# A four-layer graph network on sparse slots: two checks with earlier loads, ScalarE copies for the last groups, and another order of the drain

## The chip, the cores and the metric

The kernel runs on one core of one Trainium2 chip. The metric is the time of one execution on the device in microseconds (us). The time before is 1694.29 us, the median of three runs (1689.37 to 1699.63).

## The reference

There are 128 graphs of 64 nodes with 128 features each (`x`), and an adjacency of 64x64 weights per graph (`adj`), about a quarter of them not zero. Four layers follow each other; each is a graph network whose output is added to its input and normalised over the features.

```python
# layers 0 and 1: a filter per edge
g = exp(coeff * (d_ij - offsets)**2)          # 20 gaussians in layer 0, 64 in layer 1
W = ssp(g @ fw1 + fb1) @ fw2 + fb2            # ssp: softplus less log 2
W = W * weight(d_ij)                          # a cosine cutoff in layer 0, adj itself in layer 1
agg[i] = sum_j (x @ w_in)[j] * W[i, j]
out = ssp(agg @ ow1 + ob1) @ ow2 + ob2
# layer 2: two graph convolutions
h = elu(elu(x @ W0 + b0))
h = elu(nA @ (h @ W1) + b1)                   # nA: adj + 1, scaled by 1/sqrt(degree) on both sides
out = nA @ (h @ W2) + b2
# layer 3
out = relu((nA3 @ x) @ W.T + b)
# after each layer
x = layernorm(x + out)                        # (x - mean) / sqrt(var + 1e-5)
```

## The kernel before, in words

Two graphs make a pair: 128 nodes, one on each partition. Only edges that are there are computed. A node's edges are compacted into slots, the nodes are sorted by their number of edges, and a slot's rows go through memory so that the next step reads them in order. A count decides on the device whether the slots hold all edges; if they do not, another version of the kernel (a dense one, not touched here) runs behind a branch. Everything below is in `sparse_stack`.

**The main loop.** There are 64 pairs, and 128 loop pairs: layer 0 takes pairs 0 to 63, layer 1 pairs 8 to 63 and then 0 to 7. Each has three chunks (`for i in range(3 * N + 2)`, with `n, k = divmod(i, 3)`). For a chunk, TensorE makes the filter's first product `px` (L1753), ScalarE its gaussians and softplus (`d`, `h`), TensorE the second product `pw` (L1766) and the gather `pg` of node features by a one-hot matrix (L1779, `hot` from L1738), ScalarE copies `g` out, VectorE multiplies `m` (L1794), and VectorE sums the segments into `agg` (L1818, L1822). Behind a group of pairs come the node's own layers and a layer normalisation (L1393 to L1415).

**Groups.** Four pairs make a group (`GS`). In layer 1 groups 0 to 13 hold pairs 8 to 63, group 14 holds pairs 0 to 3, group 15 pairs 4 and 5, group 16 pair 6 and group 17 pair 7. Layers 2 and 3 follow for each group in `graph_convs` (L1655 to L1717). In the order of the work its steps are: transpose `gx` and its copy `gxt` (L1664); `gh0` and an `elu` twice over; `hw1` and its copy; `gh1` and an `elu`; `hw2` and its copy; `o2`, the sum `gz2`, a normalisation into `x_all`; `sup` and its copy; `o3`, the sum `gz3` (L1710), a normalisation, and the store. The copies behind `hw1`, `hw2` and `sup` are L1653, the two halves of `elu` are `em` (L1594, the negative part) and `er` (L1595, the positive part), both read from the same accumulator bank. Groups 14 to 17 store by one DMA of SyncE each (L1715); the others scatter four stores from GpSimd (L1719, L1028).

**The normalisation.** Per pair there is a `bn_stats` and a `bn_aggr` on VectorE (L1398, L1399). Then VectorE adds the epsilon to the variances (L1403), and the root is taken: for a group of four on GpSimd by a power of −0.5 (L1406), and for a smaller group on ScalarE by Ln and Exp. The last step, subtract and multiply (L1411), is on GpSimd for a group of four, else on VectorE.

**The order of the work.** Work beside the chunks stands in queues of Python generators; a `yield` ends a step. `run(queue, n)` takes n steps, `slot(queue)` takes one, and a step that has just issued matmuls (`yield True`) lets one more step of its queue follow after the next queue's turn. The queues are:

- `early`: the gathering of layer 1's slots, and at its end two checks (`bounded`), the sum of all checks (`settle`) and the constants of layers 2 and 3 (`late_constants`, among them 16 powers on GpSimd at L1492). It gets twelve steps per loop pair for most of layer 0;
- `side`: `spread_again`, up to two steps a chunk. It loads 16 pieces of a sorted table (`ad0again`, L1068), makes addresses of them on VectorE (`goes`, L1075), scatters rows by them on GpSimd and writes slots;
- `nodes` and two `convs`: the node layers of groups 0 to 14 and their convolutions. At the end of the loop group 14 is in `nodes` and group 13 in one of the `convs`;
- `last`: one queue each for groups 15, 16 and 17;
- `stores`: the scattered stores.

Behind the loop a drain takes what is left in the queues, one turn each: 15, 16, 17, `nodes`, the two `convs`, then one store. `in_order` pins the order of the instructions on every engine as it was written, for the loop and the drain together. So an engine that waits for one instruction holds all that was written behind it.

**Buffers.** The accumulator banks of all this node work come from one ring of two (`ps_n`, tag "n"); `st`, `mv` and `rs` of the normalisation have two buffers each. Every ScalarE activation goes through the helper `act`, and so has line L949.

In `bounded` each of two checks loads a weight and a bias, takes absolute values on VectorE (L1245), sums them by a matmul (L1249) and compares.

Of the kernel before, what the change touches and what calls it, by code (L numbers as in the profile page):

```python
# [12 lines left out]
F32 = mybir.dt.float32  # L13
AF = mybir.ActivationFunctionType
ALU = mybir.AluOpType
# [4 lines left out]
P = 128  # L20
# [6 lines left out]
LN_EPS = 1e-5  # L27
# [574 lines left out]
def sparse_stack(ctx: ExitStack, tc: tile.TileContext, t: dict, out: bass.AP, flag):  # L602
# [11 lines left out]
    nc = tc.nc  # L614
    x, adj = t["x"], t["adj"]
    NB = x.shape[0]
    NP = NB // 2
    GS = 4
    PACE = 4
# [6 lines left out]
    const = ctx.enter_context(tc.tile_pool(name="sconst", bufs=1))  # L626
# [41 lines left out]
    nc.vector.memset(half, 0.5)  # L668
    one = const.tile([P, 1], F32, name="one")
    nc.vector.memset(one, 1.0)  # L670
    neg_one = const.tile([P, 1], F32, name="neg_one")
    nc.vector.memset(neg_one, -1.0)

# [120 lines left out]
    def wait_steps(n):  # L794
        yield from (None for _ in range(n))
# [142 lines left out]
    def act(out_, in_, func, **kw):  # L938
        nonlocal fence, latest, kind
        now = func == AF.Sin  # L940
        if kind is None or now != kind:
            fence = latest
            if not now:
                ctx_ = tc.issue_after(fence.ins) if fence is not None else nullcontext()
                with ctx_:
                    fence = nc.scalar.preload_act_table_set("natural_log_exp_and_others")
            kind = now
        with tc.issue_after(fence.ins) if fence is not None else nullcontext():
            latest = nc.scalar.activation(out_, in_, func, **kw)  # L949
        return latest  # L950
# [276 lines left out]

    def spread_again(s, comb):
        yield from permuted(s, True)
        yield  # L1230
        goes_on(s)
        yield from spread(s, comb)

    def bounded():


        for i, (w, b, k) in enumerate(
            (("L0_gnn_fw1", "L0_gnn_fb1", NG0), ("L1_gnn_W1T", "L1_gnn_b1", NG1))
        ):
            w1 = big(f"w1_{i}", C)[0:k]  # L1240
            nc.sync.dma_start(w1, t[w])
            b1 = const.tile([P, 1], F32, name=f"b1_{i}")
            nc.sync.dma_start(b1, column(b))
            yield from wait_steps(PACE)
            nc.vector.scalar_tensor_tensor(w1, w1, -1.0, w1, ALU.mult, ALU.max)  # L1245
            nc.vector.scalar_tensor_tensor(b1, b1, -1.0, b1, ALU.mult, ALU.max)
            yield from wait_steps(PACE)
            u = ps_n.tile([P, 512], F32, tag="n", name=f"sum_{i}")
            nc.tensor.matmul(u[:, 0:1], lhsT=w1, rhs=one[0:k], start=True, stop=True)  # L1249
            nc.vector.tensor_add(b1, b1, u[:, 0:1])  # L1250
            nc.vector.tensor_scalar(odd[:, 1 + i : 2 + i], b1, X_LIMIT, None, ALU.is_gt)
            yield from wait_steps(PACE)
# [140 lines left out]
    def layernorm(y, dst, n, name):  # L1393

        stats = node.tile([P, GS, 6], F32, tag="st", name=f"st_{name}")[:, 0:n]
        mv = node.tile([P, GS, 2], F32, tag="mv", name=f"mv_{name}")[:, 0:n]
        for s in range(n):
            nc.vector.bn_stats(stats[:, s, :], y[:, s, :])  # L1398
            nc.vector.bn_aggr(mv[:, s, :], stats[:, s, :])  # L1399
            if s + 1 == GS // 2 < n:  # L1400
                yield
        rstd = node.tile([P, GS], F32, tag="rs", name=f"rs_{name}")[:, 0:n]
        nc.vector.tensor_scalar(rstd, mv[:, :, 1], LN_EPS, None, ALU.add)  # L1403
        yield
        if n == GS:
            nc.gpsimd.tensor_tensor(rstd, rstd, neg_half[:, 0:n], ALU.pow)  # L1406
        else:
            act(rstd, rstd, AF.Ln)
            act(rstd, rstd, AF.Exp, scale=-0.5)
        for s in range(n):  # L1410
            (nc.gpsimd if n == GS else nc.vector).tensor_scalar(  # L1411
                dst[:, s, :], y[:, s, :], mv[:, s, 0:1], rstd[:, s : s + 1],
                ALU.subtract, ALU.mult,
            )
        yield  # L1415
# [174 lines left out]
    def elu(ps, bias, i, q):  # L1590

        n = ps.shape[1] // P
        m, r = tiled(f"em{i}", n, q), tiled(f"er{i}", n, q)
        nc.vector.tensor_scalar(m, ps, bias, 0.0, ALU.add, ALU.min)  # L1594
        nc.vector.tensor_scalar(r, ps, bias, 0.0, ALU.add, ALU.max)  # L1595
        yield
        act(m, m, AF.Exp)
        if i == 0:
            act(m, m, AF.Exp, bias=neg_one)
        yield  # L1600
        nc.vector.scalar_tensor_tensor(r, m, 1.0, r, ALU.subtract, ALU.add)
        yield
        return by_pair(r)
# [12 lines left out]
    def normal(i, q, nT):  # L1616
# [7 lines left out]
        dinv = g[f"dinv{i}"][:, pairs]  # L1624
        nc.vector.tensor_mul(nT, ps, dinv.unsqueeze(2).to_broadcast([P, n, P]))

    normals = {}

    def normals_of(q):
# [10 lines left out]
    def graph_convs(q):  # L1640

        pairs = GROUPS[1][q]
        xs = x_all[:, pairs, :]
        n = xs.shape[1]

        def times(name, lhs, rhs):

            _, ps = bank(f"{name}_{q}", n)
            for s in range(n):
                nc.tensor.matmul(ps[:, s, :], lhsT=lhs(s), rhs=rhs(s), start=True, stop=True)  # L1650
            yield True
            y = by_pair(tiled(f"gy_{name}", n, q))
            nc.vector.tensor_copy(y, ps)  # L1653
            yield
            return y  # L1655

        if n == GS:
            scaled(2, q)
        flat, ps = bank(f"gx_{q}", n)
        for s in range(n):  # L1660
            nc.tensor.transpose(ps[:, s, :], xs[:, s, :], ident)
        yield True
        xt = tiled("gxt", n, q)
        nc.vector.tensor_copy(xt, flat)  # L1664
        nc.gpsimd.tensor_tensor(xs, xs, g["b2"].unsqueeze(1).to_broadcast([P, n, C]), ALU.add)
        yield
        flat, _ = bank(f"gh0_{q}", n)
        nc.tensor.matmul(flat, lhsT=g["W0"], rhs=xt, start=True, stop=True)
        yield True
        h = yield from elu(flat, g["b0"], 0, q)  # L1670
        y = yield from times("hw1", lambda s: h[:, s, :], lambda s: g["W1"])
        if n == GS:
            nT = by_pair(tiled("nTs2", n, q))
            yield from normal(2, q, nT)
            yield
        else:
            nT = normals[2, q]
        flat, ps = bank(f"gh1_{q}", n)
        for s in range(n):
            nc.tensor.matmul(ps[:, s, :], lhsT=y[:, s, :], rhs=nT[:, s, :], start=True, stop=True)  # L1680
        yield True
        h1 = yield from elu(flat, g["b1"], 1, q)
        y2 = yield from times("hw2", lambda s: h1[:, s, :], lambda s: g["W2"])
        _, ps = bank(f"o2_{q}", n)
        for s in range(n):
            nc.tensor.matmul(ps[:, s, :], lhsT=nT[:, s, :], rhs=y2[:, s, :], start=True, stop=True)
        if n == GS:
            scaled(3, q)
        yield True
        z = by_pair(tiled("gz2", n, q))  # L1690
        nc.vector.tensor_add(z, ps, xs)
        yield
        yield from layernorm(z, xs, n, f"2_{q}")
        if n == GS:
            nT3 = by_pair(tiled("nTs3", n, q))
            yield from normal(3, q, nT3)
            yield
        else:
            nT3 = normals[3, q]
        y3 = yield from times("sup", lambda s: xs[:, s, :], lambda s: nT3[:, s, :])  # L1700
        flat, ps = bank(f"o3_{q}", n)
        nc.tensor.matmul(
            flat, lhsT=ones, rhs=g["b3"][:, 0:n, :].rearrange("i s c -> i (s c)"),
            start=True, stop=False,
        )
        for s in range(n):
            nc.tensor.matmul(ps[:, s, :], lhsT=y3[:, s, :], rhs=g["W3"], start=False, stop=s == n - 1)
        yield True
        z = by_pair(tiled("gz3", n, q))
        nc.vector.scalar_tensor_tensor(z, ps, 0.0, xs, ALU.max, ALU.add)  # L1710
        yield
        yield from layernorm(z, z, n, f"3_{q}")
        if pairs.start < 8:
            b = 2 * pairs.start
            nc.sync.dma_start(out[b : b + 2 * n].rearrange("(s b) n c -> (b n) s c", b=2), z)  # L1715
        else:
            stores.append(store_rows(pairs, z))  # L1717
# [111 lines left out]

    befores, nodes, convs, sums = deque(), deque(), (deque(), deque()), deque()  # L1830
    small_groups, small = range(NP // GS - 1, len(GROUPS[1])), {}
    last = {q: deque() for q in small_groups}
    stores = deque()
    slot_data, messages, aggs = {}, {}, {}
# [122 lines left out]
        past = [c, c1]  # L1957
    run(sums, -1)
    while nodes or convs[0] or convs[1] or any(last.values()) or stores:
        for queue in (*last.values(), nodes, *convs):  # L1960
            slot(queue)
        run(stores, 1)
    in_order(before_loop, block[-1], (nc.tensor, nc.scalar, nc.vector, nc.gpsimd, nc.sync))

# [46 lines left out]
```

## Time and profile before

| what | value |
|---|---|
| median of three runs | 1694.29 us |
| the profiled execution | 1692.3 us, of it span 1690.4 us |
| PE busy | 1529.1 us (90%) |
| DVE busy | 1509.3 us (89%) |
| ACT busy | 1351.8 us (80%) |
| POOL busy | 721.1 us (43%) |
| mean TensorE clock | 0.966 of full |
| end of the last segment sum (L1822) | 1633.3 us |

PE is TensorE, DVE VectorE, ACT ScalarE, POOL GpSimd and SP SyncE; PEld is TensorE's loading of weights. L1403 is line 1403 of the kernel before. A line of a timeline gives start, length, engine, instruction, tiles and shapes, and in brackets how long the engine had been idle before it and what released it. A line of waits gives the instruction that waited, what released it, the total in us, how many there were and the mean. The page's part 2 cuts the span into 40 slices of some 42 us: a digit is the busy share in tenths, in the row PEclk the granted TensorE clock in tenths. The ends of matmuls are modelled, so a PE that is always busy is not for that reason at its limit.

### The profile page before, as it was taken

How to read it: one execution, taken by the hardware profiler on the slowest of the kernel's cores; microseconds unless marked ns; L12 is line 12 of the kernel's file. 1: busy time of each engine (PE TensorE's matmuls, PEld its weight loads, DVE VectorE, ACT ScalarE, POOL GpSimd, SP SyncE). 2: the span in 40 equal slices, each digit the busy share in tenths (PEclk: the TensorE clock that was granted, in tenths of full speed). 3: DMA queues.
4: the chain of work that ended last, by engine and by line, in shares of the span. 5: the costliest groups of instructions: out<-in, count | busy, mean ns of one | idle time of the engine just before them, and what ended most of it. 6: DMA issues, size and time to landing. Idle time of an engine off the chain costs nothing.

```text
span 1690.4 us, 24016 instructions
## 1 busy us (share of the span) xinstructions
PE 1529.1 (90%) x6813; PEld 790.9 (47%) x6813; DVE 1509.3 (89%) x4125; ACT 1351.8 (80%) x1699; POOL 721.1 (43%) x1119
## 2 busy tenths in 40 slices
PE   1289999999889999998999999999999999998975
PEld 1134444444444444454444555555555555544444
DVE  7689999999979999789888999999999999988875
ACT  1369898989788989697999888898898888887831
POOL 2424455444645433133412354444554444554344
PEclk9999999999989999798999999999999999999986
DMA  7656554556454544344666465555465455465100
GB/s 253 197 127 144 126 139 119 130 125 157 117 123 120 142 114 116 90 130 106 150 149 133 116 144 128 119 134 134 114 141 126 114 133 125 115 143 131 45 6 21
DMA packets 119055, 211.22 MB, mean 125 GB/s; under 512 B 46830, under 2 KB 70656, under 8 KB 118272
## 3 DMA queue, kind: packets, MB, share of 16 engines
q1 hardware_dynamic: 107760, 193.11, 47.6%
q0 software_dynamic: 6576, 14.99, 2.8%
q10 hardware_dynamic: 4576, 1.49, 0.4%
q8 instruction: 56, 0.92, 0.2%
q14 instruction: 87, 0.71, 0.2%
HBM read 190.86 MB, written 18.64 MB: 124 GB/s over the span
## 4 chain that ended last, share of the span: by engine, by line
PE 32%; DVE 11%; issue 8%; POOL 7%; DMA 6%; ACT 4%; SPq 1%; DVEq 0%; POOLq 0%; ACTq 0%
PE pw L1766 11%; PE pg L1779 7%; PE px L1753 6%; DMA out_dram<-gz,at_row 5%; POOL x_all L1411 3%; DVE m L1794 3%; DVE agg L1818 2%; POOL rs L1406 1%; ACT h L949 1%; POOL gz L1411 1%; PE hw L1650 1%; DVE hot L1738 1%; ACT d L949 1%; ACT g L949 1%; PE back L1577 1%
## 5 line engine op out<-in xcount | busy, mean ns | idle before, releaser
L949 ACT ACTIVATE g<-pg 128x672 f32<-128x672 f32 (+12 forms) x384 | 298.8, 778 | 134.3 <-PE pg L1779 129.4
L949 ACT ACTIVATE h<-h,half 128x672 f32<-128x672 f32 (+13 forms) x385 | 351.1, 912 | 12.5
L1779 PE MATMUL pg<-hot,ys 64*128 64x336 f32 (+12 forms) x1536 | 352.6, 537 | 4.7 <-ACT g L949 4.6
L1818 DVE TENSOR_REDUCE agg<-m 128x16 f32<-128x240 f32 (+13 forms) x896 | 324.8, 410 | 2.4
L1766 PE MATMUL pw<-h,w_L_gnn_fw 128*128 128x336 f32 (+6 forms) x768 | 279.6, 489 | 38.9 <-DVE m L1794 38.8
L1766 PE MATMUL pw<-h,w_L_gnn_W2T 128*128 128x420 f32 (+5 forms) x768 | 303.1, 517 | 3.0 <-DVE m L1794 3.0
L1794 DVE SCALAR_TENSOR_TENSOR m<-pw,c_L_gnn_b,g 128x420 f32<-128x420 f32 (+5 forms) x384 | 226.0, 625 | 10.9 <-PE pw L1766 8.1
L1794 DVE SCALAR_TENSOR_TENSOR m<-pw,c_L_gnn_fb,g 128x336 f32<-128x336 f32 (+6 forms) x384 | 201.9, 564 | 25.9 <-PE pw L1766 19.6
L949 ACT ACTIVATE h<-px,c_L_gnn_b 128x840 f32<-128x840 f32 (+5 forms) x192 | 176.8, 921 | 44.6 <-PE px L1753 44.3
L1779 PEld LDWEIGHTS pg<-hot,ys 64*128 64x128 f32 x1536 | 118.6, 189 | 187.3 <-ACT h L949 98.9
L1766 PEld LDWEIGHTS pw<-h,w_L_gnn_fw 128*128 128x128 f32 x768 | 138.6, 199 | 135.8 <-DVE m L1794 84.7
L1753 PE MATMUL px<-d,fw 32*128 32x336 f32 (+6 forms) x768 | 170.8, 522 | 29.5 <-ACT d L949 28.6
L1766 PEld LDWEIGHTS pw<-h,w_L_gnn_W2T 128*128 128x128 f32 x768 | 133.1, 191 | 129.3 <-DVE m L1794 32.3
L1406 POOL TENSOR_TENSOR rs<-rs,neg_half 128x4 f32<-128x4 f32 x61 | 67.8, 1111 | 276.8 <-DVE rs L1403 275.4
L1738 DVE SCALAR_TENSOR_TENSOR hot<-j,row,w 128x1212 f32<-128x1212 bf16 (+12 forms) x128 | 175.7, 1373 | 8.8 <-DMA w<-w_dram 8.8
L949 ACT ACTIVATE h<-px,c_L_gnn_fb 128x672 f32<-128x672 f32 (+6 forms) x192 | 158.3, 824 | 20.8 <-PE px L1753 15.6
L1753 PE MATMUL px<-d,w1t 64*128 64x420 f32 (+5 forms) x768 | 169.8, 519 | 0.0
L949 ACT ACTIVATE d<-d,neg_off 128x1212 f32<-128x1212 f32 (+12 forms) x128 | 136.4, 1065 | 8.0 <-DMA d<-d_dram 8.0
L1028 POOL DMA_INDIRECT rows<-comb,goes x64 | 68.9, 1076 | 117.7 <-DMA rows<-comb,goes 75.9
L1753 PEld LDWEIGHTS px<-d,fw 32*128 32x128 f32 x768 | 60.3, 191 | 124.8 <-issue 46.9
L1411 POOL TENSOR_SCALAR x_all<-ny,mv,rs 128x128 f32<-128x128 f32 x124 | 108.5, 881 | 3.4
L1028 POOL DMA_INDIRECT out_dram<-gz,at_row x56 | 71.3, 1273 | 50.5 <-DMA out_dram<-gz,at_row 39.8
(261 smaller groups left out, 2206.6 us busy)
## 6 DMA issues: line engine op xcount, KB each, us to landing
d<-d_dram SPq DMA_DIRECT2D x32, 315.0 KB
w<-w_dram SPq DMA_DIRECT2D x32, 315.0 KB
d<-d_dram SPq DMA_DIRECT2D x32, 303.0 KB
w<-w_dram SPq DMA_DIRECT2D x32, 303.0 KB
w<-w_dram SPq DMA_DIRECT2D x32, 252.0 KB
j<-j_dram SPq DMA_DIRECT2D x32, 157.5 KB
j<-j_dram SPq DMA_DIRECT2D x32, 151.5 KB
d<-d_dram SPq DMA_DIRECT2D x16, 300.0 KB
```

The source lines that it names most:

```text
L949: latest = nc.scalar.activation(out_, in_, func, **kw)
L1028: nc.gpsimd.indirect_dma_start(out=into, out_offset=bass.IndirectOffsetOnAxis(ap=at, axis=0), in_=rows, in_offset=None,)
L1406: nc.gpsimd.tensor_tensor(rstd, rstd, neg_half[:, 0:n], ALU.pow)
L1411: (nc.gpsimd if n == GS else nc.vector).tensor_scalar(dst[:, s, :], y[:, s, :], mv[:, s, 0:1], rstd[:, s : s + 1], ALU.subtract, ALU.mult,)
L1577: nc.tensor.matmul(ps[:, s, :], lhsT=back[:, s, :], rhs=o[:, s, :], start=True, stop=True)
L1650: nc.tensor.matmul(ps[:, s, :], lhsT=lhs(s), rhs=rhs(s), start=True, stop=True)
L1738: nc.vector.scalar_tensor_tensor(hots[n][:, 0:size], j[:, 0:size], near, wt[:, 0:size], ALU.is_equal, ALU.mult)
L1753: nc.tensor.matmul(ps[:, b, 0:n], lhsT=w["w1"][rows, :], rhs=d[rows, col : col + n], start=True, stop=True,)
L1766: nc.tensor.matmul(ps[:, 0 : c["size"]], lhsT=c["w"]["w2"], rhs=c["h"][:, b, :], start=True, stop=True)
L1779: nc.tensor.matmul(ps[:, b, 0:n], lhsT=y[rows, :], rhs=hots[c["n"]][rows, at], start=True, stop=True,)
L1794: nc.vector.scalar_tensor_tensor(messages[n][:, b, at], c["pw"][b][:, 0:size], c["w"]["b2"], c["g"][:, b, :], ALU.add, ALU.mult,)
L1818: nc.vector.tensor_reduce(av[:, :, :, r], both, AX.X, ALU.add)
```

## The change

Five edits, without any in the number of matmuls, loads or stores:

1. `spread_again` lets four steps pass between its loads and `goes`, not one.
2. `bounded` issues the loads of both checks first, lets 32 steps of `early` pass, and then makes the two checks, with eight steps between the absolute values and the sum, not four. It takes 56 steps, not 24, and what stands behind it in `early` moves back.
3. The addition of the epsilon leaves VectorE. For groups of four GpSimd does it, ahead of its power; for smaller groups it is the bias of ScalarE's Ln, from a constant tile. The 70 instructions of L1403 become 61 on GpSimd.
4. For groups 14 to 17 (`at_end`) the four copies (`gxt`, `hw1`, `hw2`, `sup`) and the positive half of both `elu` go from VectorE to ScalarE: 24 instructions.
5. In the drain, the queue of group 17 has a turn ahead of each other queue that isn't empty, and one more at the end of each round.

```diff
     def spread_again(s, comb):
         yield from permuted(s, True)
-        yield
+        yield from wait_steps(4)
         goes_on(s)
         yield from spread(s, comb)
 
     def bounded():
+        loaded = []
         for i, (w, b, k) in enumerate(
             (("L0_gnn_fw1", "L0_gnn_fb1", NG0), ("L1_gnn_W1T", "L1_gnn_b1", NG1))
         ):
...
             nc.sync.dma_start(b1, column(b))
-            yield from wait_steps(PACE)
+            loaded.append((w1, b1))
+        yield from wait_steps(8 * PACE)
+        for i, (w1, b1) in enumerate(loaded):
             nc.vector.scalar_tensor_tensor(w1, w1, -1.0, w1, ALU.mult, ALU.max)
             nc.vector.scalar_tensor_tensor(b1, b1, -1.0, b1, ALU.mult, ALU.max)
-            yield from wait_steps(PACE)
+            yield from wait_steps(2 * PACE)
             u = ps_n.tile([P, 512], F32, tag="n", name=f"sum_{i}")
...
         rstd = node.tile([P, GS], F32, tag="rs", name=f"rs_{name}")[:, 0:n]
-        nc.vector.tensor_scalar(rstd, mv[:, :, 1], LN_EPS, None, ALU.add)
         yield
         if n == GS:
+            nc.gpsimd.tensor_scalar(rstd, mv[:, :, 1], LN_EPS, None, ALU.add)
             nc.gpsimd.tensor_tensor(rstd, rstd, neg_half[:, 0:n], ALU.pow)
         else:
-            act(rstd, rstd, AF.Ln)
+            act(rstd, mv[:, :, 1], AF.Ln, bias=ln_eps)
             act(rstd, rstd, AF.Exp, scale=-0.5)
...
         nc.vector.tensor_scalar(m, ps, bias, 0.0, ALU.add, ALU.min)
-        nc.vector.tensor_scalar(r, ps, bias, 0.0, ALU.add, ALU.max)
+        if q in at_end:
+            act(r, ps, AF.Relu, bias=bias)
+        else:
+            nc.vector.tensor_scalar(r, ps, bias, 0.0, ALU.add, ALU.max)
...
+    def copy(to, ps, q):
+        if q in at_end:
+            act(to, ps, AF.Copy)
+        else:
+            nc.vector.tensor_copy(to, ps)
...
-            nc.vector.tensor_copy(y, ps)
+            copy(y, ps, q)
...
-        nc.vector.tensor_copy(xt, flat)
+        copy(xt, flat, q)
...
     small_groups, small = range(NP // GS - 1, len(GROUPS[1])), {}
+    at_end = range(NP // GS - 2, len(GROUPS[1]))
...
     while nodes or convs[0] or convs[1] or any(last.values()) or stores:
-        for queue in (*last.values(), nodes, *convs):
-            slot(queue)
+        longest = last[small_groups[-1]]
+        for queue in (*list(last.values())[:-1], nodes, *convs):
+            if queue:
+                slot(longest)
+                slot(queue)
+        slot(longest)
         run(stores, 1)
```

More of the change, by code (lines that the diff above doesn't have):

```diff
@@ L670, in sparse_stack @@
     nc.vector.memset(one, 1.0)
+    ln_eps = const.tile([P, 1], F32, name="ln_eps")
+    nc.vector.memset(ln_eps, LN_EPS)
     neg_one = const.tile([P, 1], F32, name="neg_one")
@@ L1243, in bounded @@
             nc.sync.dma_start(b1, column(b))
-            yield from wait_steps(PACE)
+            loaded.append((w1, b1))
+        yield from wait_steps(8 * PACE)
+        for i, (w1, b1) in enumerate(loaded):
             nc.vector.scalar_tensor_tensor(w1, w1, -1.0, w1, ALU.mult, ALU.max)
             nc.vector.scalar_tensor_tensor(b1, b1, -1.0, b1, ALU.mult, ALU.max)
-            yield from wait_steps(PACE)
+            yield from wait_steps(2 * PACE)
             u = ps_n.tile([P, 512], F32, tag="n", name=f"sum_{i}")
-            nc.tensor.matmul(u[:, 0:1], lhsT=w1, rhs=one[0:k], start=True, stop=True)
+            nc.tensor.matmul(u[:, 0:1], lhsT=w1, rhs=one[0 : w1.shape[0]], start=True, stop=True)
             nc.vector.tensor_add(b1, b1, u[:, 0:1])
```

## The prediction

> **What bounds the kernel now.** I read the page first, then the waits by engine, the busy time by stage, and the timeline at the few places where an engine stands still.
>
> ```profile
> PE 1529.1 (90%) x6813; PEld 790.9 (47%) x6813; DVE 1509.3 (89%) x4125; ACT 1351.8 (80%) x1699; POOL 721.1 (43%) x1119
> ...
> PEclk9999999999989999798999999999999999999986
> ...
> PE 32%; DVE 11%; issue 8%; POOL 7%; DMA 6%; ACT 4%; SPq 1%; DVEq 0%; POOLq 0%; ACTq 0%
> ```
>
> TensorE and VectorE are both near 90%, and the clock row dips at slices 12 and 17 and at the end. The busy time by stretch (columns: window; length, PE, PEld, DVE, ACT, POOL busy with instructions; clock, DMA share, GB/s) tells the stages apart:
>
> ```profile
> 480.00:500.00 20.00, 15.11 (x66) 7.26 (x64) 12.99 (x38) 15.03 (x19) 8.61 (x11) 0.83 0.63 144
> 695.00:720.00 25.00, 22.76 (x91) 11.03 (x90) 17.38 (x47) 17.23 (x24) 0.96 (x1) 0.80 0.28 69
> 1000.00:1200.00 200.00, 199.77 (x928) 106.53 (x928) 187.75 (x427) 174.37 (x204) 90.19 (x97) 1.00 0.55 127
> 1632.00:1684.00 52.00, 34.18 (x147) 24.57 (x147) 36.08 (x127) 9.91 (x33) 21.40 (x26) 0.70 0.05 14
> ```
>
> In the steady loop (row 3) PE shows 199.8 of 200 us and DVE 187.8; PE's ends are modelled, and in the timeline it keeps being released by DVE's product `m` (L1794), so I take DVE as the tight engine there. Rows 1 and 2 are two short stalls; row 4 is the tail, where nothing is full and a chain decides.
>
> **The two stalls.** The timeline has them (columns: start, length, engine and instruction, then the idle time before it and its releaser):
>
> ```profile
> 488.70 0.23 DVE L1075 TENSOR_SCALAR goes<-ad0again,row 128x8 uint32<-128x8 f32 x1 [6.76 <-DMA ad0again<-perm_again]
> ...
> 490.06 2.61 PE L1766 MATMUL pw<-h,w_L_gnn_fw 128*128 128x336 f32 x4 [4.89 <-DVE m L1794]
> ```
>
> ```profile
> 697.95 0.28 DVE L1245 SCALAR_TENSOR_TENSOR w<-w 20x128 f32<-20x128 f32 x1 [4.69 <-DMA w<-in_L_gnn_fw_dram]
> 698.29 0.30 PE L1249 MATMUL sum<-one,w 20*128 20x1 f32 x1 [2.24 <-DVE w L1245]
> 699.65 2.58 PE L1766 MATMUL pw<-h,w_L_gnn_fw 128*128 128x332 f32 x4
> ```
>
> DVE takes its queue in order, so a `goes` or a `w` that waits for its load holds the `m` behind it. After the gap the same four matmuls take 2.61 and 2.58 us; at 482.33 they took 1.30.
>
> **What the Trainium skill says.** "TensorE: Matmul & The Clock Gate", Part 1 (HAM clock gate): after an idle window of about 3.4 us PE runs at half clock until about 3.4 us of activity. The trace agrees: 1.30 to 2.61 us after an idle of 4.89, and to 2.58 at the second stall. "Perfetto Trace Analysis", Optimizing Scalar/DVE Operations: each DVE or ScalarE instruction has a fixed access overhead; work may be moved from a saturated DVE to ScalarE, but between GpSimd and DVE it may not help, since they share an SBUF port. The trace shows the overhead (128x4 add, 0.2 us a slot); the port sharing it doesn't show. "PSUM — Partial Sum Buffer", PSUM bank collisions: accesses of one bank by two engines must be serialised. The trace agrees: DVE's `nh` (L1556) waits 38.9 us in 24 cases for ScalarE's `na` on the same bank.
>
> **The change, part by part.** Sums are against the profiled execution, 1692.3 us (span 1690.4, 1.9 around it); it lies 2.0 under the shown median of 1694.3.
>
> *Checks further ahead.* `goes<-ad0again` goes about three chunks later (some 12 us at about 4 us a chunk), `w` eight chunks later: both exceed the 6.76 and 4.69 us by which the loads were late. SP's sixteen loads (5.67 us of issue) keep their place, and DVE work of the next chunks covers them. The scatters, row loads and stores behind `goes` move by up to a pair (13 us); POOL's `dinv` powers (16, last start 822.5) move by up to three chunks, and their first use is at 897.6. First stall: stepping through the order without that wait, the `m` that came at 493.06 could come at about 487.2: 5.9 us. Cover against it: ScalarE's two table loads (1.28 us each, 483.4 and 485.1) in the same gap, so 2.6 less at worst. Second: 2.24 us of PE idle, plus some 5.3 us that PE's groups take longer at half clock until 708 (L1766 1.3 more, L1779 and L1753 0.65 more a group), less what DVE makes up: 6. Sum −12 (−6 to −16).
>
> *L1403.* By shape, 61 adds of 128x4 are busy 20.1 us, mean 329 ns (a few long ones); by start times one occupies 0.2 us of DVE: from an aggregate (1245.86) over its add (1246.08) to the next instruction (1246.16) it is 0.30, and 0.10 where no add follows (1628.10 to 1628.20). 56 of the 61 lie in the loop: 56 × 0.2 = 11.2. The group of four pairs is DVE-paced, but not everywhere: I take −9 (0 if PE is the limit, to −14 where slots are 0.25). POOL gets 61 adds ahead of the power. That form isn't in the trace; POOL's small TENSOR_SCALARs (L1094, 128x13) have a median of 0.25, its 128x128 one 0.78: I take 0.4 and both as bounds. POOL has 90 of 200 us, so in the loop it is hidden; in the tail five of them lie on the chain. The small groups' add goes into ScalarE's Ln: nine DVE slots of 0.08 to 0.2, near nothing.
>
> *Copies and `er` on ScalarE.* 24 instructions leave DVE in the tail: gxt .68+.41+2×.28, `er` 2×(.74+.47+2×.34), hw 2×(.69+.42+2×.28), sup .69+.39+2×.28, in all 10.6 us, to a ScalarE with 9.9 of 52 us busy. `er` now waits for `em` (same bank) and the exponential behind it comes 0.3 to 0.6 later; for a chain this is nearly neutral. It frees DVE, which the drain uses: counted below. One wait is new on DVE: group 16's third mean takes one of two `mv` buffers, which POOL's `x_all` of group 14 gives back; behind it on DVE stands group 14's last stage, which needs that `x_all` too, so I cost it at nothing (up to 3 us, one POOL normalisation, if it catches group 16's end).
>
> *The drain.* In the built order all of the last pair's work (queue 17) now stands ahead of group 13's last norm on DVE, ScalarE and PE. Before, from the last segment sum (L1822, ending 1633.3) to that norm it was 16.6 us:
>
> ```profile
> 1649.88 1.03 POOL L1406 TENSOR_TENSOR rs<-rs,neg_half 128x4 f32<-128x4 f32 x1 [2.12 <-DVE rs L1403]
> ...
> 1666.49 3.19 POOL L1411 TENSOR_SCALAR x_all<-gz,mv,rs 128x128 f32<-128x128 f32 x4
> ...
> 1670.57 0.69 DVE L1653 COPY gy_sup<-sup 128x512 f32<-128x512 f32 x1 [3.10 <-PE sup L1650]
> ...
> 1677.86 1.03 POOL L1406 TENSOR_TENSOR rs<-rs,neg_half 128x4 f32<-128x4 f32 x1 [8.18 <-DVE rs L1403]
> 1679.00 3.12 POOL L1411 TENSOR_SCALAR gz<-gz,mv,rs 128x128 f32<-128x128 f32 x4
> ```
>
> From there POOL runs a chain of its own to the end, 40.5 us: group 13's four normalisations and four stores (3.2 us apart), group 14's power, its `x_all`, PE's sup, o3, its second power and `gz`, then the store. Queue 17 alone, summed over its rows: DVE 6.9, ScalarE 4.1, PE some 5.5 (eleven stages at 0.4 to 0.8), with 33 handovers of 0.05 to 0.1: 19 to 20 us, and with the work of others between, 21 to 26. So group 13's norm comes +5 to +10 later. What follows gets shorter by about 3: the copy of sup beside DVE, and 17's end (DVE's 1.47 wait, ln, `gz`, 1683.4) no longer behind POOL. The last sum itself ends 1 earlier (gxt copies of .68 and .41 gone from in front). Adds on POOL: +1. +7 −3 −1 +1 ≈ +4 to +5. I take +5 (−4 to +9). What ends last then is group 14 through POOL.
>
> Sum: −12 −9 +5 = −16, hence 1676 for the profiled execution and about 1678 for the median.
>
> **Rivals.** (a) *The loop is PE-bound.* For: 199.8 of 200. Against: its ends are modelled, and it waits 41.8 us for `m`. Then L1403 gives 0, the stalls about 6, the tail takes 5: 1693, no change. (b) *The tail gains.* For: 17 was last, 10.6 us leave DVE. Against: POOL's 40.5 us hold no 17. If group 13's norm doesn't move and the −3, −1 stand with 4 more: −12 −9 −8 → 1665. (c) *Slower.* The turns of 17 put group 13's norm, and with it POOL's serial chain, behind 17's handovers at half clock (0.70 here): 14 later instead of 7, tail +12, and the loop gives 3 or less: 1703. It decides where the tail's loss is over the loop's gain by 8.5. (d) *The checks still wait*, because layer 1's `goes` meets other late loads: −12 becomes −3, so 1687: no change.
>
> **Chances.** Forecast (1670 to 1686) 0.5; (b) 0.14; (a) and (d) 0.21; (c) 0.15. Faster, by over 0.5%, which is about what can be told from no change, means under 1685.8: 0.5 and 0.14, less the forecast's edge: 0.63; same 0.22; slower 0.15. The range leaves (c) and a little of (b) out: 1664 to 1697.
>
> **What would show it.** No wait of DVE for `ad0again` or `w`, and a clock near 1.0 in slices 12 and 17; L1403 gone from DVE and the groups of four pairs in the loop shorter by 0.2 us a norm; 17's store ahead of group 13's and POOL's last `gz` ending last; a tail of about 62 us from the last sum, against 57.1. Wrong would be: a loop of the old length, a new wait of POOL or DVE in the loop, or a tail over 66 us.

## The result, and the profile after

The changed kernel takes 1687.75 us (median of 18 runs), the kernel before 1698.0 us over as many. The ratio is 0.9942, 95% interval 0.9921 to 0.9962: about 10 us are gained, where 16 were forecast. The time lies just above the forecast of 1670 to 1686 and within the wider 1664 to 1697; the sum does not hold, since its terms are off in both directions. The profiled execution has a span of 1686.6 us, against 1690.4.

The page of the changed kernel, the lines that answer to those shown of before (line numbers in a view are those of the kernel that it shows):

```profile
PE 1517.6 (90%) x6813; PEld 788.5 (47%) x6813; DVE 1480.2 (88%) x4032; ACT 1359.3 (81%) x1723; POOL 737.2 (44%) x1180
...
PEclk9987999999989999999999999999999999999965
...
PE 46%; DVE 22%; DMA 9%; ACT 7%; POOL 7%; issue 5%; SPq 2%; another core or an unknown queue 1%; DVEq 0%; POOLq 0%; ACTq 0%
```

DVE has 93 instructions and 29 us less. The clock row's dips in slices 17 and 19 are gone, that in slice 12 is not; slices 3 and 4 and the last two are slower. The two checks no longer wait for their loads.

To see where the time went I cut the execution by loop pairs: the start of each pair's one-hot instruction (`hot`) in DVE's timeline marks them, the end of the last `agg` marks the last segment sum, and the tail is the rest of the span. Lengths in us:

| kernel | pairs 0-8 | 8-34 | 34-38 | 38-50 | 50-56 | 56-60 | 60-64 | 64-120 | 120 to last sum | tail |
|---|---|---|---|---|---|---|---|---|---|---|
| before | 99.0 | 289.4 | 50.9 | 129.1 | 72.1 | 38.1 | 49.3 | 695.7 | 133.8 | 57.1 |
| changed | 106.6 | 280.6 | 51.1 | 128.6 | 61.8 | 38.3 | 46.8 | 697.0 | 129.8 | 70.1 |

The 75.9 us ahead of pair 0 are the same in both. Before the last sum 16.8 us are gained, although pairs 0 to 8 took 7.6 more. I leave these pairs out, since they do not follow the change: of the executions below, with the edits and without them, some show 94 to 99 us there and others 102 to 108. The tail loses 13.0.

Much of what differs between the two rows is PE's clock. The same stretches, as the time in us for which the clock stood at one half (worked out from the granted clock of windows of some 4 us, as length × 2 × (1 − clock)):

| kernel | pairs 0-8 | 8-34 | 34-38 | 38-50 | 50-56 | 56-60 | 60-64 | 64-120 | 120 to last sum | tail |
|---|---|---|---|---|---|---|---|---|---|---|
| before | 3.4 | 13.7 | 13.6 | 3.4 | 17.1 | 0 | 13.7 | 0 | 13.3 | 36.6 |
| changed | 27.3 | 0 | 17.0 | 0 | 3.5 | 0 | 3.4 | 0 | 11.3 | 56.5 |

From pair 8 to the last sum that is 74.8 us before and 35.2 changed. The same four matmuls take 2.61 us at half clock and 1.30 at full clock, so 39.6 us less at half clock are worth up to 20 us, by estimate, of the 24.4 that these stretches gained. So a wait that goes can save more than its own length: the slow matmuls behind it go too.

**The tail.** POOL's and SP's lines of the changed kernel's timeline, from its last segment sum at 1616.5 on:

```profile
1643.77 0.34 SPq L1730 DMA_DIRECT2D out_dram<-gz  x1
...
1646.15 0.23 POOL L1410 TENSOR_SCALAR rs<-mv 128x4 f32<-128x4 f32 x1 [3.48 <-DVE mv L1404]
1646.47 1.04 POOL L1411 TENSOR_TENSOR rs<-rs,neg_half 128x4 f32<-128x4 f32 x1
...
1663.04 1.05 POOL L1411 TENSOR_TENSOR rs<-rs,neg_half 128x4 f32<-128x4 f32 x1
1664.19 3.13 POOL L1416 TENSOR_SCALAR x_all<-gz,mv,rs 128x128 f32<-128x128 f32 x4
...
1673.68 0.23 POOL L1410 TENSOR_SCALAR rs<-mv 128x4 f32<-128x4 f32 x1 [6.36 <-DVE mv L1404]
```

Queue 17's store is issued first, 27.3 us after the last sum, and group 13's last norm begins right behind it, at 29.6 us where it was 16.6. From there to the end it is 40.4 us, and it was 40.5: POOL's chain has moved as a whole.

**The first check.** The stretch of pairs 34 to 38 gained nothing in this execution, though DVE no longer waits for `ad0again`:

```profile
483.90 3.16 SPq L1070 DMA_DIRECT2D ad0again<-perm_again  x8
...
487.18 1.42 SPq L1290 DMA_DIRECT2D d<-d_dram  x3
...
490.55 0.85 ACT L951 ACTIVATE d<-d,neg_off 96x672 f32<-96x672 f32 x1 [4.15 <-DMA d<-d_dram]
...
492.07 1.11 PE L1794 MATMUL pg<-hot,ys 64*128 64x336 f32 x4 [3.90 <-ACT g L951]
...
494.52 2.61 PE L1781 MATMUL pw<-h,w_L_gnn_fw 128*128 128x336 f32 x4
```

SP issues the loads of `d` behind those of `ad0again`. ScalarE waits 4.15 us for `d` (1.92 in the kernel before), PE stands still for 3.90, and its clock halves as it did before (2.61 for the four matmuls). This wait alone did not eat the gain. The same kernel with the old drain (e1 below) has nearly the same wait, and its stretch takes 45.8 us. Its lines:

```profile
490.86 0.86 ACT L951 ACTIVATE d<-d,neg_off 96x672 f32<-96x672 f32 x1 [3.86 <-DMA d<-d_dram]
...
492.38 1.49 PE L1794 MATMUL pg<-hot,ys 64*128 64x336 f32 x4 [3.61 <-ACT g L951]
...
499.75 1.40 PE L1781 MATMUL pw<-h,w_L_gnn_fw 128*128 128x336 f32 x4
```

In the changed kernel the same matmuls are still slow much later:

```profile
507.15 2.45 PE L1781 MATMUL pw<-h,w_L_gnn_fw 128*128 128x336 f32 x4
```

The clock was back at about 499 in e1, after 6.8 us, and at about 509 in the changed kernel, after 17.0, although PE's row has no gap there from 492 on. Why it took so much longer is open.

### The profile page after: what moved, and what is told of

Same layout as the page of the kernel before. It is cut to its first block, busy times and chain, and to the rows that moved or that the text cites. A ratio compares the mean times of both kernels' runs of the same rounds, so it can differ in the third digit from the quotient of the medians.

```text
span 1686.6 us, 24029 instructions
## 1 busy us (share of the span) xinstructions
PE 1517.6 (90%) x6813; PEld 788.5 (47%) x6813; DVE 1480.2 (88%) x4032; ACT 1359.3 (81%) x1723; POOL 737.2 (44%) x1180
## 4 chain that ended last, share of the span: by engine, by line
PE 46%; DVE 22%; DMA 9%; ACT 7%; POOL 7%; issue 5%; SPq 2%; another core or an unknown queue 1%; DVEq 0%; POOLq 0%; ACTq 0%
PE pw L1781 16%; PE pg L1794 9%; PE px L1768 9%; DVE m L1809 6%; DMA out_dram<-gz,at_row 5%; DVE agg L1833 3%; ACT h L951 2%; POOL gz L1416 2%; DVE hot L1753 2%; PE y L1441 2%; ACT g L951 2%; POOL x_all L1416 2%; DMA w<-w_dram 1%; ACT d L951 1%; DVE at L1179 1%
## 5 line engine op out<-in xcount | busy, mean ns | idle before, releaser
L1781 PE MATMUL pw<-h,w_L_gnn_fw 128*128 128x336 f32 (+6 forms) x768 | 273.1, 479 | 29.3 <-DVE m L1809 26.5
L1410 POOL TENSOR_SCALAR rs<-mv 128x4 f32<-128x4 f32 x61 | 25.9, 425 | 266.8 <-DVE mv L1404 265.5
L1416 POOL TENSOR_SCALAR x_all<-ny,mv,rs 128x128 f32<-128x128 f32 x124 | 104.9, 855 | 3.3
L1768 PEld LDWEIGHTS px<-d,w1t 64*128 64x128 f32 x768 | 68.6, 187 | 49.3 <-issue 11.9
```

What stands on the lines that cost most here:

```text
L1410: nc.gpsimd.tensor_scalar(rstd, mv[:, :, 1], LN_EPS, None, ALU.add)
L1416: (nc.gpsimd if n == GS else nc.vector).tensor_scalar(dst[:, s, :], y[:, s, :], mv[:, s, 0:1], rstd[:, s : s + 1], ALU.subtract, ALU.mult,)
L1768: nc.tensor.matmul(ps[:, b, 0:n], lhsT=w["w1"][rows, :], rhs=d[rows, col : col + n], start=True, stop=True,)
L1781: nc.tensor.matmul(ps[:, 0 : c["size"]], lhsT=c["w"]["w2"], rhs=c["h"][:, b, :], start=True, stop=True)
```

## The experiments

My theory after the result had four parts: the drain's turns cost the tail 10 us and more by putting off group 13's norm; the checks give the loop's gain; the moved addition gives nothing in layer 1, since PE paces it; the ScalarE copies give nothing. The rivals stand with each run. Lengths of stretches, tails and times at half clock come from one profiled execution of each kernel. Ratios are to the kernel before, with their 95% intervals.

**Old drain (e1).** The changed kernel with the drain of before:

```diff
-        longest = last[small_groups[-1]]
-        for queue in (*list(last.values())[:-1], nodes, *convs):
-            if queue:
-                slot(longest)
-                slot(queue)
-        slot(longest)
+        for queue in (*last.values(), nodes, *convs):
+            slot(queue)
```

> The changed kernel with the drain's order of before; the other four edits stay. Theory (the turns of queue 17 put its chain ahead of group 13's last norm, and with it the whole POOL chain): from the last segment sum to the end of the span it is about 56 us again, where the changed kernel has 70.1 and the kernel before 57.1; the time is about 13 us under the changed kernel's, ratio to the kernel before about 0.986. Rival (the loss of the tail comes from `er` waiting for `em` on another engine, the ScalarE copies and POOL's added step): the tail stays at 68 to 70 us and the ratio at 0.994.

The tail is 58.1 us and the ratio 0.9882 (0.9839 to 0.9925). Group 13's norm comes at 17.2 us after the last sum, and 41.0 follow:

```profile
1633.35 0.23 POOL L1410 TENSOR_SCALAR rs<-mv 128x4 f32<-128x4 f32 x1 [1.45 <-DVE mv L1404]
```

So the drain's order gives away some 10 us of what the rest of the change gains.

**Drain alone (e8).** The kernel before with the reverse of that edit.

> The kernel before with the new drain alone. Theory: the tail goes from 57.1 to 67 to 71 us, with the loop as before: ratio 1.006 to 1.008. Rival (the turns cost only together with the ScalarE copies, which wait for `em`): the tail stays under 61 us, ratio 1.000 to 1.002.

The tail is 67.9, the norm comes at 27.8, the ratio is 1.005 (1.0029 to 1.007). The turns cost without the ScalarE copies too. In all, the five executions with this drain have tails of 67.9 to 70.1 us (the changed kernel, e2, e4, e5 and e8), and the five with the old drain and POOL's norms 57.1 to 60.6 (the kernel before, e1, e3, e6 and e9).

**Extra turns only behind group 13 (e12).** The changed kernel with:

```diff
             if queue:
-                slot(longest)
+                if not convs[1]:
+                    slot(longest)
                 slot(queue)
```

> The changed kernel, but queue 17's extra turns begin only once group 13's queue is empty; until then each queue has one turn. Theory (the loss comes from group 13's last norm standing behind queue 17's chain, so POOL's chain begins late): that norm comes again about 17 us after the last segment sum and the tail takes 56 to 60 us, ratio 0.988. Rival (the extra turns cost by their handovers wherever they stand, or delay group 14 just as much): the tail stays at 66 to 70 us, ratio 0.994.

The norm comes at 15.6 us, the tail is 60.6, the ratio 0.9866 (0.9826 to 0.9906). So it is the place in front of group 13's norm that costs most. A smaller part of the rival is seen too, as POOL's next norm in this kernel shows:

```profile
1642.95 0.23 POOL L1410 TENSOR_SCALAR rs<-mv 128x4 f32<-128x4 f32 x1 [5.47 <-DVE mv L1404]
```

POOL now waits for group 14's mean, which the extra turns delay; from group 13's norm to the end it is 45.0 us, not 41.

**Checks alone (e3).** The kernel before with edits 1 and 2.

> The kernel before with edits 1 and 2 alone (both checks' loads further ahead). Theory (all that the loop gained comes from the second check and what moved with it; the first check's stall was replaced by ScalarE's wait for `d`): 12 to 16 us less than before, ratio 0.991 to 0.993; the tail stays at 57 us; in the stretch of loop pairs 34 to 50 nothing is gained. Rival (half of the loop's gain comes from DVE's relief): 5 to 8 us less, ratio 0.996.

The ratio is 0.9896 (0.9858 to 0.9934), a gain of some 18 us (11 to 24), which has room for the theory's 12 to 16. But one part of the expectation falls: pairs 34 to 38 take 46.2 us, not 50.9. Of all kernels with edit 1, only the profiled execution of the changed one shows no gain there (the others take 43.5 to 47.7 us, with 3.4 to 10.2 at half clock). Pairs 50 to 56 take 60.5 (72.1 and 68.2 in the two executions without edit 2), with no time at half clock (17.1 and 10.3), and pairs 60 to 64 take 47.3 (49.3). The tail is 60.6, not 57.

**Second check alone (e9).** The kernel before with edit 2.

> The kernel before with edit 2 alone (the check of the weights). Theory (the first check is worth about 5 us, the second 10 and more): loop pairs 34 to 38 take 51 us as before, where they take 44 to 46 with edit 1; pairs 50 to 56 take 60 to 63, against 72.1; ratio 0.992 to 0.994, against 0.990 with both edits. Rival (edit 1 is worth nothing, since ScalarE's wait for `d` takes the stall's place): the ratio equals that of both edits, 0.990.

The ratio is 0.9957 (0.994 to 0.9974), pairs 34 to 38 take 49.7, and 50 to 56 take 61.9. Edit 2 is worth about 7 us, and edit 1 the difference to 0.9896: some 10, with an uncertainty of about 7. The ratio is above the 0.992 to 0.994 expected: the theory had given the second check the larger share.

**Loads two to a step (e4).** The changed kernel with a `yield` between the pairs of loads:

```diff
             for k in range(8):
+                if again and k:
+                    yield
                 for h in range(2):
```

> The changed kernel, but the sixteen loads of `ad0again` (and of `ad1again`) are issued two to a step, not sixteen at once, so that SyncE can issue the loads of the next pairs' `d` between them. Theory (SyncE's queue, held by the sixteen loads and their scatters, had delayed `d`; ScalarE's 4.15 us wait for it took the place of DVE's 6.76): that wait falls under 1 us, PE keeps its clock, and 4 to 8 us are gained on the changed kernel, ratio 0.990 to 0.992. Rival (the transfer itself is late, not its issue, or another wait follows): the ratio stays at 0.994.

A miss: ScalarE's wait for `d` is gone in pairs 34 to 38, but they take 46.6 us, no less than 45.8 with the old drain alone, and the ratio is 0.9971 (0.9951 to 0.999). Another wait came instead: at 479 us PE stands still for 3.27 for an `agg` of the node layers, and its clock is at one half for 6.8 us, as long as in e1. So the run does not tell what the order of issue alone is worth there. Pairs 8 to 34 take 291.8 us, where the other kernels with the addition on POOL take 280.4 to 280.8. PE is at half clock for 20.5 of these 291.8 and for none in the others, which by estimate is 10 of the 11 us; why the spread loads bring this about stays open.

**Addition back on DVE (e2).** The changed kernel with L1403 in its old place:

```diff
+        nc.vector.tensor_scalar(rstd, mv[:, :, 1], LN_EPS, None, ALU.add)
         yield
         if n == GS:
-            nc.gpsimd.tensor_scalar(rstd, mv[:, :, 1], LN_EPS, None, ALU.add)
             nc.gpsimd.tensor_tensor(rstd, rstd, neg_half[:, 0:n], ALU.pow)
         else:
-            act(rstd, mv[:, :, 1], AF.Ln, bias=ln_eps)
+            act(rstd, rstd, AF.Ln)
```

> The changed kernel with the addition of the epsilon back on DVE, in its old place, for all groups. Theory (layer 1's loop is paced by PE, which hardly ever waits for `m` there; the 61 adds had been free): the stretch of layer 1 from loop pair 64 to 120 is as long as in the changed kernel within 2 us, and the ratio stays at 0.994. Rival (DVE paces it): that stretch grows by 8 us and the ratio goes to 0.999.

Pairs 64 to 120 take 695.4 us, against 697.0 with the addition on POOL, and 695.1 to 700.0 in all executions but e5's, on whichever engine it is: the 37 adds were free there. The ratio is 0.9965 (0.9943 to 0.9988), in between and apart from neither. What there is lies elsewhere: pairs 8 to 34 take 284.1 (280.6), pair 120 to the last sum 134.6 (129.8). In layer 0 PE does wait for `m`, a little longer with the addition on DVE, and in one place its clock then halves. The same four matmuls in e2 and, with the addition on POOL, in e1:

```profile
411.11 2.64 PE L1781 MATMUL pw<-h,w_L_gnn_fw 128*128 128x340 f32 x4 [1.44 <-DVE m L1809]
```

```profile
409.25 1.41 PE L1781 MATMUL pw<-h,w_L_gnn_fw 128*128 128x340 f32 x4 [1.02 <-DVE m L1809]
```

Pairs 8 to 34 have 3.4 us at half clock in e2, and none with the addition on POOL (e4 apart).

**A matmul twice (e5).** The changed kernel with layer 1's `u` issued twice for groups of four:

```diff
-        nc.tensor.matmul(
-            u, lhsT=w["o1"], rhs=agg.rearrange("f s r -> f (s r)"), start=True, stop=True
-        )
+        for _ in range(1 + (layer == 1 and n == GS)):
+            nc.tensor.matmul(
+                u, lhsT=w["o1"], rhs=agg.rearrange("f s r -> f (s r)"), start=True, stop=True
+            )
```

> The changed kernel, with the first matmul of layer 1's node layers (`u`, 128x512, 0.59 us) issued twice for the 15 groups of four; the second overwrites the first with the same values. About 13 of them lie between loop pairs 64 and 120: 7.7 us more for PE, nothing more for DVE. Theory (PE paces layer 1's loop): that stretch, 697.0 us in the changed kernel and 695.7 in the kernel before, grows by 6 to 8 us and the whole by 8 to 9, ratio 0.999. Rival (DVE paces it, or both have slack behind some latency): the stretch stays within 2 us and the ratio at 0.994.

Pairs 64 to 120 take 707.3 us, 10.3 more, and the ratio is 0.9999 (0.9972 to 1.0025). That is more than the 7.7 expected: a group's `u` is two records of together 1.12 us, and doubled it takes 1.98, so the thirteen in this stretch add 11.2. PE paces layer 1: its added work shows almost in full, DVE's did not. The page of the kernel before had said so, in two lines of its costliest groups (the last columns: idle time before them, and who ended it):

```profile
L1766 PE MATMUL pw<-h,w_L_gnn_fw 128*128 128x336 f32 (+6 forms) x768 | 279.6, 489 | 38.9 <-DVE m L1794 38.8
L1766 PE MATMUL pw<-h,w_L_gnn_W2T 128*128 128x420 f32 (+5 forms) x768 | 303.1, 517 | 3.0 <-DVE m L1794 3.0
```

`fw` is layer 0's weight, `W2T` layer 1's. Of PE's 41.8 us of waits for `m`, 38.8 are in layer 0.

**Copies back on DVE (e6).** The changed kernel with the old drain and `at_end` empty:

```diff
-    at_end = range(NP // GS - 2, len(GROUPS[1]))
+    at_end = ()
```

> The changed kernel with the drain of before and with the last groups' copies and `er` on DVE as before; what is left of the change is the checks and the moved addition. Theory (in the tail DVE's 10.6 us were no limit; POOL's chain is): the tail from the last segment sum stays at 57 to 60 us as in the run with the old drain alone (58.1), ratio 0.987 to 0.990. Rival (the copies on ScalarE did help by some 5 us): the tail is 62 us or more and the ratio 0.991 or more.

The tail is 60.5 us, against 58.1, and the ratio 0.9878 (0.9847 to 0.9909), against 0.9882. The copies are worth nothing that can be told: DVE had 25.7 us of work in the 50.8 from the last sum on in e1, and the two tails also differ in their time at half clock (50.4 and 44.4).

**Last norms off POOL (e10).** The changed kernel with the old drain, and:

```diff
+        on_pool = n == GS and name not in ("3_13", "2_14", "3_14")
         yield
-        if n == GS:
+        if on_pool:
...
-            (nc.gpsimd if n == GS else nc.vector).tensor_scalar(
+            (nc.gpsimd if on_pool else nc.vector).tensor_scalar(
```

> The changed kernel with the drain of before, and the last norm of group 13 and both last norms of group 14 done as the small groups' are (Ln and Exp on ScalarE, the last step on DVE), not on POOL. Theory (POOL's serial chain sets the tail; DVE takes 0.3 us a pair where POOL takes 0.8, and group 14 no longer waits for group 13's stores): the tail goes from 58 to 49 to 53 us, ratio 0.983 to 0.985. Rival (another chain, that of queue 17 or of group 14 through PE at half clock, ends as late): 56 us or more, ratio 0.987 to 0.988.

The tail is 52.9 us and the ratio 0.9813 (0.9777 to 0.9849), the lowest of all: 1656 us, where the kernel before took 1690 beside it. The interval of e1 reaches down to 0.9839, so the time alone does not part the two; the tail, shorter than the 57.1 to 60.6 of the five above, does. The theory's way is seen in part: group 14's norm does not get past group 13's stores but still comes behind the last of them, the first line below, and what is shorter is the step itself:

```profile
1641.09 0.96 POOL L1030 DMA_INDIRECT out_dram<-gz,at_row  x1 [2.08 <-DVE gz L1726]
...
1642.21 1.11 DVE L1417 TENSOR_SCALAR x_all<-gz,mv,rs 128x128 f32<-128x128 f32 x4 [0.86 <-ACT rs L951]
...
1652.97 1.11 DVE L1417 TENSOR_SCALAR gz<-gz,mv,rs 128x128 f32<-128x128 f32 x4 [0.17 <-ACT rs L951]
...
1656.79 0.35 DVE L1417 TENSOR_SCALAR gz<-gz,mv,rs 128x128 f32<-128x128 f32 x1 [0.60 <-ACT rs L951]
```

Four pairs take DVE 1.11 us, where POOL took 3.13, twice over, and group 14's last stage is done at 1654.1, which is 44.2 us after the last sum, against 49.8 in e1; what ends last now is a small group again. PE was at half clock for only 29.0 us of this tail (44.4 in e1), and what part of the 5 us that is, the run does not show.

**Groups 13 and 14 first in a round (e11).** As e10, with `for queue in (*convs, nodes, *last.values())`.

> As the run before it (three norms off POOL), with the drain's turns in the order convs, nodes, then queues 15, 16, 17. Theory (groups 13 and 14 set the end, so their turn should be first in a round): one more turn's lead, 1 to 3 us less, ratio 0.982 to 0.985. Rival (a round's order doesn't matter, since every queue has one turn in it): the same as the run before it.

A miss: the tail is 54.7 us, the ratio 0.9842 (0.9804 to 0.9881), no better than e10. A round's order is not worth a turn, as the rival said.

## Why the prediction was off, point by point

Two steps of the prediction failed: that DVE is the tight engine of the steady loop, and that queue 17 puts group 13's norm off by only 5 to 10 us. A third term, that of the checks, was too small. Of the signs of being wrong that the prediction named, a tail over 66 us came (70.1).

- *Two checks, −12 forecast.* The mechanism holds, the size was low: −17.7 by the time of both alone (0.9896 of 1698.0). 7 are the second check's, where 6 were forecast. The first gives more than the 5.9 of its stall; part of it lies in pairs 8 to 34, which take 284.6 with both edits and 286.8 to 290.9 without edit 1. The sum priced only the wait for `ad0again`, and for this check none of the slow matmuls behind a wait: without edit 1 PE is at half clock for 6.9 to 13.7 us in pairs 8 to 34 and for 13.6 in pairs 34 to 38, with both edits alone for 3.4 and 6.8. Edit 1 also moves the `goes` of `ad1again`, which begins at 185.0 before and 202.7 after; that this makes the difference in pairs 8 to 34 I have not tested. A gain of 2 at pairs 60 to 64 wasn't foreseen either (46.6 to 47.3 us with edit 1, but 50.0 in e1; 49.3 without).
- *L1403, −9 forecast.* The step "I take DVE as the tight engine there" failed. The −9 priced the 56 adds of the loop as if DVE paced nearly all of it, from a wait summed over both layers. PE paces layer 1, and the 37 adds of pairs 64 to 120 gave 0. What the addition gives (0.9942 against 0.9965, 4 us with an uncertainty of more than 4) shows in layer 0 and the last pairs. Rival (a) was right on this term, but not on the stalls.
- *POOL's added step, 0.4 assumed:* it took 0.23 us in the lines above and 0.425 in the mean of all 61, a few being long, and no loss shows in the loop.
- *ScalarE copies:* the forecast put no number to them but in the −3 behind the norm. The chain from POOL's `rs` of group 14 to its next got 1.6 us shorter (12.52 to 10.95), and the stores ahead of it 1.1 longer (15.46 to 16.57 between the powers): 40.4 for 40.5. The −3 was not there. The sum of the 24 instructions, given as 10.6 us, is 10.4 by its own terms; nothing hangs on it.
- *The drain, +5 forecast for the tail, +13.0 measured.* The mechanism was right: group 13's norm stood behind queue 17, and POOL's chain began later. The term "+5 to +10 later", taken at 7, was too small; it was 13.0, near the mechanism of rival (c), which had 14. The loop's gain covered it: that the total still came within 6 us of the forecast is luck, since errors of both signs met.

Why 27.3 us for queue 17, which I had at 19 to 20 alone and 21 to 26 with others between? Two lines of busy time, from the last sum to group 13's norm, before and changed (columns as in the prediction):

```profile
1633.30:1649.90 16.60, 12.10 (x64) 8.60 (x64) 12.20 (x39) 4.81 (x14) 1.27 (x3) 0.89 0.01 1
```

```profile
1616.50:1646.20 29.70, 20.43 (x82) 15.12 (x82) 13.93 (x44) 11.42 (x34) 2.98 (x6) 0.61 0.01 2
```

DVE did 1.7 us more in 13.1 us more, PE 8.3 more, and its clock fell from 0.89 to 0.61. A chain of one pair leaves the engines idle at each handover, and between two turns of queue 17 there still is one of another queue, in order, with instructions four pairs wide. In the changed kernel's timeline:

```profile
1629.15 1.91 PE L1665 MATMUL sup<-nTs,x_all 128*128 128x128 f32 x8
1630.86 0.64 PE L1695 MATMUL gh<-small,gy_hw 128*128 128x128 f32 x2
1631.10 0.69 DVE L1640 COPY gy_sup<-sup 128x512 f32<-128x512 f32 x1 [1.80 <-PE sup L1665]
1631.71 0.34 DVE L1599 TENSOR_SCALAR em<-gh,c_L_gnn_b 128x128 f32<-128x128 f32 x1
```

Queue 17's `gh` waits behind 1.91 us of another group's `sup`, and its `em` behind the copy of that. The prediction had taken PE's stages at 0.4 to 0.8 us and the handovers at 0.05 to 0.1; the order's waits and the halved clock were the missing part. Two of the experiments help to part them. Up to group 13's norm PE is at half clock for 14.1 us both in e3, with the old drain, and in e8, with the new one, and the norm comes at 19.7 and 27.8 us: about 8 us are the order's. The other 5 go along with the clock, which up to the norm is at one half for 3.7 us in the kernel before (norm at 16.6) and for 22.8 in the changed kernel (29.6). Each of these is one execution.

The terms as measured, −18 for the checks, −2 to −4 for the addition (e1 against e3, and e2 against the changed kernel), 0 for the copies, +8.5 to +10 for the drain (e8: +0.5% of 1698.0; changed less e1: 0.6%), make −10 to −13.5; −10 was measured. Each term is uncertain by some us, so this says no more than that they are compatible.

## What to carry to other kernels

Split a wait by stage before naming the engine that paces a stage: the total had 41.8 us, and 38.8 of them were in the other layer. Price a stall of PE with the matmuls at half clock behind it: at the second stall of the kernel before PE stood still for 2.24 us, and 10.3 us at half clock followed (698.4 to 708.7). When a queue is to be drained first, ask what now stands behind it in order on each engine, and whether that feeds the slower chain; the queue that ended last was not the one that set the end, since POOL's chain of 40 us began with another group. Here the serial tail was shortened by taking work off its slow engine (52.9 us, against 58.1), and by no other order of turns.

## What the runs showed that I had not expected

How long PE's clock stays at one half does not follow from how busy PE is. In the changed kernel's tail it stayed at 0.50 from 1617 to 1632 us, with PE busy for 10.8 of these 15 us and no wait of more than 1.6 us:

```profile
1617.00:1622.00 5.00, 3.77 (x8) 1.68 (x7) 2.09 (x6) 2.38 (x7) 1.51 (x2) 0.50 0.00 0
1622.00:1627.00 5.00, 3.22 (x12) 2.44 (x12) 1.94 (x6) 2.90 (x9) 0.46 (x1) 0.50 0.00 0
1627.00:1632.00 5.00, 3.80 (x15) 3.21 (x15) 2.47 (x8) 1.24 (x4) 0.00 (x0) 0.50 0.00 0
1632.00:1637.00 5.00, 3.98 (x27) 3.39 (x28) 1.74 (x7) 1.71 (x5) 0.00 (x0) 0.94 0.00 0
```

It returned where the matmuls came close together (27 in the last window). The Trainium skill ("TensorE: Matmul & The Clock Gate", Part 1) has the clock return after about 3.4 us of activity; here activity with gaps of up to 1.54 us was not enough. Nor was activity without gaps at all times: in pairs 34 to 38 of the changed kernel PE's row is full from 492 to 509 us, and the clock came back only at its end. It takes no idle window of 3.4 us to lose the clock either: it halved after a wait of 1.44 in e2 and of 2.24 at the second stall of the kernel before, which the prediction counted as agreement. What does agree is a length of about 3.4 us: in pairs 8 to 64 the times at half clock lie near its multiples (3.4, 6.8, 10.2, 13.7, 17.0, 20.5). What decides how many of them a wait costs, these runs do not show.

A chain of single steps, as in this tail, pays for its handovers and for matmuls at half clock.
